# One static order for all engines, and two operands of a two-layer convolution block made by TensorE products instead of a copy through DRAM

## The chip, the core and the metric

The kernel runs on one NeuronCore of a Trainium2 chip. The metric is the device time of one execution in microseconds (us). The core has a matrix engine (TensorE, PE in the profile; its weight loads are listed as PEld), VectorE (DVE), ScalarE (ACT), GpSimd (POOL) and SyncE (SP), which here issues the DMA transfers. [...]

## What is computed

The input x is 32 samples of 96 channels of 56 x 56 values in f32. Two layers follow each other, each with a group normalisation in front (32 groups of 3 channels) and x added at the end.

```python
# layer 0: an inverted bottleneck with 4-bit weights and activations
h = act_q(bn(conv1x1(x, quant_w(w1)) ))          # 96 -> 576 channels
h = act_q(bn(depthwise3x3(h, quant_w(w2))))      # 576
h = bn(conv1x1(h, quant_w(w3)))                  # 576 -> 96
x = x + (gn(x) + h)
# layer 1: three branches of 32 channels, gated by small MLPs of the channels' means
x_0  = group_conv3x3(x_0, conv0_w * Y0)                       # spatial
Mix  = group_conv1x1(frft2d(x_05, alpha), conv05_w * Y)       # fractional Fourier, real and imaginary
x_05 = abs(frft2d(Mix, -alpha)) / (H * W)
x_1  = irfft2(group_conv1x1(rfft2(x_1), conv1_w * Y1))        # Fourier
x = x + conv3x3(concat(x_0, x_05, x_1), conv2_w) + conv2_b    # 96 -> 96
```

## The kernel before

The samples are worked one after the other, with layer 1 of one sample running beside layer 0 of the next. Line numbers are those of the profile.

Layer 0 of a sample. `norm` (L330) takes the channel statistics of x in seven pieces (L333) and `group_stats` (L290) turns them into mean and scale. `split` (L345) writes the normalised x as a high and a low part (`vh`, `vl`). `expand` (L368) makes 128 of the 576 channels at one of four pixel phases: four products on PE (L372), then `quant_act` (L310), in which ScalarE evicts the bank pair to integers (L313) and VectorE clips (L315), then up to four DMAs (L385) that bring the result into the padded buffer `qp`. There are 20 such steps. `depthwise` (L390) is eight fp8 products (L398) for 32 channels with all four phases, and again `quant_act`; 18 such steps. `project` (L407) goes back to 96 channels (L414) and adds to x (L426).

Layer 1 of a sample. `means`, `gates`, `weights` and `angles` (L454 to L605) compute the gates, the sample's own weights `g0`, `g1` and `g2`, and the transform matrices `cs`, a long chain of small steps over PE, VectorE and ScalarE. `mix_t` (L608) and `hilbert` (L624) are the Fourier branch, `spatial` (L722) is the 3 x 3 branch. The fractional branch is the one that the change touches. `mix_f` (L644) multiplies x of that branch by `g1` (`pm`, L653) and gets 128 rows: 64 of them (here called p and q) still have to be transformed, the other 64, called a0 and b0, do not. All 128 go to DRAM (`z`, L658). From there two transfers bring p and q back laid out by image row (`zh`, L663), and eight bring a0 and b0 back laid out by four rows (`az`, L671). `rows_f` (L673) transforms along rows into `Y`, `columns_f` (L694) along columns into the bank `pz` (L702); VectorE adds `az` (L712), ScalarE squares (L713), VectorE adds real and imaginary part into `Z` (L715), and `magnitude` (L717) takes the root into the concatenated image `cat` (L720). `final` (L742) is the last 3 x 3 convolution: for each of seven blocks of eight image rows nine products, called taps, of 96 x 448 from `cat` into one bank (`pc`, L746), then VectorE adds them to x (L754). The profile counts an f32 product as two records.

The order. `interleave` (L87) merges two lists of steps, of layer 0 and of layer 1 of the sample before, by weights written beside each step. The steps are whole functions, so the nine taps of a block stand together. The framework's own scheduler, run with a simulated timeline, may then rearrange instructions. Tiles come from pools with few buffers: two bank pairs for `expand`, `depthwise` and `project`, four single banks for everything else, three buffers for the integers of `quant_act`, three of the clipped `q1s`.

Of the kernel before, what the change touches and what calls it, by code (L numbers as in the profile page):

```python
# [49 lines left out]
NB = 5  # L51
# [12 lines left out]
LEAD = 7  # L64
# [22 lines left out]
def interleave(a, b):  # L87

    ta, tb = sum(c for c, _ in a) or 1, sum(c for c, _ in b) or 1
    i = j = 0  # L90
    ca = cb = 0.0
    while i < len(a) or j < len(b):
        if j >= len(b) or (i < len(a) and ca * tb <= cb * ta):
            ca += a[i][0]
            a[i][1]()
            i += 1
        else:
            cb += b[j][0]
            b[j][1]()
            j += 1  # L100
# [3 lines left out]
def block_kernel(ctx: ExitStack, tc: tile.TileContext, out: bass.AP, a: dict):  # L104
# [5 lines left out]
    xp = ctx.enter_context(tc.tile_pool(name="xp", bufs=3))  # L110
    p1 = ctx.enter_context(tc.tile_pool(name="p1", bufs=1))
    p2 = ctx.enter_context(tc.tile_pool(name="p2", bufs=2))
    p3 = ctx.enter_context(tc.tile_pool(name="p3", bufs=3))
    dp = ctx.enter_context(tc.tile_pool(name="dp", bufs=2, space=bass.MemoryType.DRAM))
    ps0 = ctx.enter_context(tc.tile_pool(name="ps0", bufs=2, space=PSUM))
    ps1 = ctx.enter_context(tc.tile_pool(name="ps1", bufs=4, space=PSUM))

    def bank(pool, name):
        return pool.tile([128, 512], F32, tag="bank", name=name)

    def pair(name):

        return ps0.tile([128, 2, 512], F32, tag="pair", name=name)


    xts = {}

    def load(i):
        xt = xp.tile([C, HW], F32, tag="x", name=f"x{i}")
        nc.sync.dma_start(out=xt, in_=x_in[i].rearrange("c h w -> c (h w)"))  # L130
        xts[i] = xt

    load(0)


# [6 lines left out]
    gmat = const("gmat")  # L142
    def prepare():

        room = p1.tile([128, NG0 * PN // 2], F32, tag="q2", name="prep")
# [107 lines left out]
    for k in range(3):  # L253
        t = cp.tile([128, PH, PW], FP8, tag=f"q1s{k}", name=f"q1s{k}")
        nc.gpsimd.memset(t, 0.0)
        q1s.append(t)
# [17 lines left out]
    bcoef = p1.tile([128, 128], F32, tag="vv", name="bcoef")  # L274
    g1 = cp.tile([128, 128], F32, tag="g1", name="g1")
# [5 lines left out]
    g2 = cp.tile([128, 128], F32, tag="g2", name="g2")  # L281
    nc.vector.memset(g2, 0.0)
    cs = cp.tile([LOW + W, 2 * W], F32, tag="cs", name="cs")
    nc.vector.memset(cs, 0.0)
    zh = cp.tile([LOW + W, G, LOW], F32, tag="zh", name="zh")
    nc.gpsimd.memset(zh, 0.0)
    Y = cp.tile([LOW + W, H, G], F32, tag="Y", name="Y")
    nc.gpsimd.memset(Y, 0.0)

    def group_stats(stats, name):  # L290

        mv = p2.tile([C, 2], F32, tag="mv", name=f"mv{name}")
        nc.vector.bn_aggr(mv, stats)
        pm = bank(ps1, f"pm{name}")
        nc.tensor.matmul(pm[:C, 0:1], gmat, mv[:, 0:1], start=True, stop=True)
        st = p2.tile([C, 4], F32, tag="st", name=f"st{name}")
        mean, rstd, gap, d = (st[:, k : k + 1] for k in range(4))
        nc.vector.tensor_copy(mean, pm[:C, 0:1])
        nc.vector.tensor_tensor(d, mv[:, 0:1], mean, ALU.subtract)
        t = p2.tile([C, 1], F32, tag="gt", name=f"gt{name}")  # L300
        nc.vector.scalar_tensor_tensor(t, d, d, mv[:, 1:2], ALU.mult, ALU.add)
        pv = bank(ps1, f"pv{name}")
        nc.tensor.matmul(pv[:C, 0:1], gmat, t, start=True, stop=True)
        ve = p2.tile([C, 1], F32, tag="ve", name=f"ve{name}")
        nc.vector.tensor_scalar(ve, pv[:C, 0:1], 1e-5, None, ALU.add)
        nc.gpsimd.tensor_tensor(rstd, ve, mhalf, ALU.pow)
        nc.vector.tensor_tensor(gap, d, rstd, ALU.mult)
        return mean, rstd, gap

    def quant_act(ps, scale, offset, dst, name):  # L310

        t = p3.tile([128, PN], I16, tag="qt", name=f"qt{name}")
        nc.scalar.activation(t.rearrange("p (h n) -> p h n", h=2), ps[:, :, :HN], AF.Relu, bias=offset, scale=scale)  # L313
        src = t if len(dst.shape) == 2 else t.rearrange("p (h w) -> p h w", w=PH)
        nc.vector.tensor_scalar(dst, src, 15.0, None, ALU.min, saturate=False if dst.dtype == FP8 else None)  # L315

    stats2 = {}
    turn = {"q1s": 0}


    def phase(xt, k, rows=PH):

        return view(xt, W * (k // 2) + k % 2, [[2 * W, PH], [2, PH]])

    def layer0(i):

        xt = xts[i]
        s = {}

        def norm():  # L330
            stats = p2.tile([C, NCH, 6], F32, tag="bn", name=f"bn{i}")
            for j in range(NCH):
                nc.vector.bn_stats(stats[:, j, :], xt[:, j * CN : (j + 1) * CN])  # L333
            mean, rstd, _ = group_stats(stats.rearrange("p c s -> p (c s)"), f"a{i}")
            s["mean"], s["rstd"] = mean, rstd
            stats2[i] = p2.tile([C, NCH, 6], F32, tag="bn2", name=f"bn2{i}")

            t = p2.tile([C, 3], F32, tag="aff", name=f"aff{i}")
            nmr, s["one"], s["off"] = (t[:, k : k + 1] for k in range(3))
            nc.vector.scalar_tensor_tensor(nmr, mean, -1.0, rstd, ALU.mult, ALU.mult)  # L340
            nc.vector.tensor_scalar(s["one"], rstd, 1.0, None, ALU.add)
            nc.vector.tensor_tensor(s["off"], nmr, B3, ALU.add)
            s["nmr"] = nmr

        def split(k):  # L345
            src = phase(xt, k)
            if k == 0:
                s["vh"] = p1.tile([C, 4, PN], F32R, tag="vh", name=f"vh{i}")
                s["vl"] = p1.tile([C, 4, PN], F32R, tag="vl", name=f"vl{i}")
            for h in range(2):  # L350
                at = slice(HN * h, HN * (h + 1))
                v = p3.tile([C, HN], F32, tag="qt", name=f"v{i}_{k}_{h}")
                nc.vector.tensor_scalar(  # L353
                    v.rearrange("p (h w) -> p h w", w=PH),
                    src[:, PH // 2 * h : PH // 2 * (h + 1), :],
                    s["mean"],
                    s["rstd"],
                    ALU.subtract,
                    ALU.mult,
                )  # L360
                nc.scalar.copy(s["vh"][:, k, at], v)  # L361
                nc.vector.tensor_tensor(s["vl"][:, k, at], v, s["vh"][:, k, at].bitcast(F32), ALU.subtract)

        def base():

            nc.vector.tensor_scalar(xt, xt, s["one"], s["off"], ALU.mult, ALU.add)

        def expand(b, k):  # L368
            ps = pair(f"pe{i}_{b}_{k}")
            for n, v in enumerate((s["vh"], s["vl"])):  # L370
                for h in range(2):
                    nc.tensor.matmul(  # L372
                        ps[:, h, :HN],
                        w1[:, 128 * b : 128 * (b + 1)],
                        v[:, k, HN * h : HN * (h + 1)],
                        start=(n == 0),
                        stop=(n == 1),
                    )
            src = q1s[turn["q1s"] % 3]
            turn["q1s"] += 1  # L380
            quant_act(ps, A1[:, b : b + 1], B1[:, b : b + 1], src[:, :, :PH], f"e{i}_{b}_{k}")

            n, at = blk(b) // G, PW * (k // 2) + k % 2
            for g in range(n):
                nc.sync.dma_start(  # L385
                    out=qps[(NB * i + b) % 3][G * k : G * (k + 1), g, at : at + PH * PW],
                    in_=src[g * G : (g + 1) * G].rearrange("c h w -> c (h w)"),
                )

        def depthwise(b, j):  # L390
            g = 4 * b + j
            if g == 0:
                s["q2"] = p1.tile([128, NG0, PN], BF16, tag="q2", name=f"q2_{i}")
            ps = pair(f"pd{i}_{g}")
            for t in range(4):
                for h in range(2):
# [4 lines left out]
                        view(qps[(NB * i + b) % 3][:, j, :], at, [[PW, PH // 2], [1, PH]]),  # L401
# [3 lines left out]
            quant_act(ps, A2[:, g : g + 1], B2[:, g : g + 1], s["q2"][:, g, :], f"d{i}_{g}")  # L405

        def project(h, lo, hi):  # L407

            if lo == 0:
                s["pp"] = [pair(f"pp{i}_{h}_{u}") for u in range(2)]  # L410
            for g in range(lo, hi):
                for k in range(4):
                    rows = slice(G * k, G * (k + 1))
                    nc.tensor.matmul(  # L414
                        s["pp"][k // 2][:C, k % 2, :HN],
                        w3[rows, g, :],
                        s["q2"][rows, g, HN * h : HN * (h + 1)],
# [3 lines left out]
            if hi < NG0:  # L421
                return
            for k in range(4):
# [4 lines left out]
        def stats():  # L428
            for j in range(NCH):
                nc.vector.bn_stats(stats2[i][:, j, :], xt[:, j * CN : (j + 1) * CN])  # L430
# [542 lines left out]
```

## Time and profile before

| | |
|---|---|
| time, median of 3 runs | 4759.75 us (4745.85 to 4771.58) |
| span of the profiled run | 4750.5 us, mean granted TensorE clock 0.941 |
| final convolution, L746, on PE | 1620.7 us busy, 4032 records |
| depthwise, L398, on PE | 956.8 us busy, 4608 records |
| expand, L372, on PE | 786.4 us busy (434.7 + 351.7), 2560 records |
| evictions of both, L313, on ACT | 1212.3 us busy (635.9 + 576.4) |
| statistics of x, L333, on DVE | 121.1 us busy, 133.6 us idle before them until x had landed |
| DMA | 249.58 MB, 53 GB/s; issues of `qp` 2304, `z` 256, `az` 256, `zh` 64 |

How to read it: "busy" is time in which an engine executes something. A busy PE is not PE at its peak, since the ends of its pipelined products are modelled and since a throttle may grant it half of its clock; the clock row of the page tells. In the list of waits a line names who waited and for whom, then the total in us, the number of times and the longest.

### The profile page before, as it was taken

The numbers are of one execution on the slowest core, as the hardware profiler recorded it, in microseconds if no ns is written. First come the engines' busy times: TensorE is split into PE (matmuls) and PEld (weight loads), VectorE is DVE, ScalarE is ACT, GpSimd is POOL, SyncE is SP. The second block draws the span as 40 slices with busy tenths as digits, with TensorE's granted clock in tenths as the row PEclk, the third lists the DMA queues.
The fourth block names the chain that finished last, engine by engine and source line by source line (L and its number), as shares of the span: only waits on it lengthen the run. The fifth ranks groups of instructions, "written<-read, shape, count | busy, mean of one in ns | idle before, by whom it ended". The sixth has DMA issues, their size and how long they took to land.

```text
span 4750.5 us, 59888 instructions
## 1 busy us (share of the span) xinstructions
PE 4293.0 (90%) x21632; PEld 2471.1 (52%) x21632; DVE 2393.3 (50%) x5385; ACT 2177.6 (46%) x2824; POOL 176.7 (4%) x209
## 2 busy tenths in 40 slices
PE   3799999999998999999999999999999999999987
PEld 2545555545555555555555555455555555555544
DVE  5545545545445455455454455454454554555532
ACT  3534445444455444455444454444454444554431
POOL 1000000000000000000000000000000000000000
PEclk9899999999999999999999999999999999999998
DMA  2212222211223211222211222122222112222112
GB/s 72 44 48 45 42 61 65 64 46 39 48 62 65 62 38 36 59 64 65 58 40 39 58 65 64 43 42 48 62 65 63 35 39 58 65 64 53 33 34 48
DMA packets 397243, 249.58 MB, mean 53 GB/s; under 512 B 283233, under 2 KB 390100, under 8 KB 390804
## 3 DMA queue, kind: packets, MB, share of 16 engines
q1 hardware_dynamic: 394368, 242.76, 23.0%
q8 instruction: 172, 2.82, 0.3%
q10 hardware_dynamic: 2580, 2.99, 0.2%
q14 instruction: 123, 1.01, 0.1%
HBM read 92.90 MB, written 89.92 MB: 38 GB/s over the span
## 4 chain that ended last, share of the span: by engine, by line
PE 63%; DVE 14%; DMA 11%; ACT 6%; issue 4%; SPq 3%; POOL 0%; DVEq 0%; ACTq 0%; POOLq 0%
PE pc L746 31%; PE pd L398 12%; PE pp L414 5%; DMA zh<-z 4%; PE pe L372 4%; PE pm L653 4%; DMA qp<-q1s 3%; PE pi L678 3%; ACT cat L720 2%; SPq L385 2%; DMA z<-zs 2%; DVE bn L333 2%; DVE q1s L315 2%; DVE x L426 2%; DMA x<-in_x_dram 1%
## 5 line engine op out<-in xcount | busy, mean ns | idle before, releaser
L746 PE MATMUL pc<-cat,wc 96*96 96x448 f32 x4032 | 1620.7, 557 | 60.9 <-ACT cat L720 60.9
L746 PEld LDWEIGHTS pc<-cat,wc 96*96 96x96 f32 x4032 | 664.1, 168 | 895.5 <-issue 809.0
L398 PE MATMUL pd<-qp,dw 128*128 128x392 fp8e4 x4608 | 956.8, 353 | 43.0 <-ACT qtd L313 37.9
L313 ACT ACTIVATE qtd<-pd,o,s 128x784 int16<-128x784 f32 x576 | 576.4, 1001 | 908.1 <-PE pd L398 878.2
L313 ACT ACTIVATE qte<-pe,o,s 128x784 int16<-128x784 f32 x640 | 635.9, 998 | 685.3 <-PE pe L372 669.5
L398 PEld LDWEIGHTS <-dw 128*128 128x128 fp8e4 x4608 | 447.4, 102 | 502.2 <-issue 203.9
L372 PE MATMUL pe<-vh,w1r 96*128 96x392 f32 x1280 | 434.7, 422 | 71.1 <-DVE x L426 41.2
L315 DVE TENSOR_SCALAR q1s<-qte 128x784 fp8e4<-128x784 int16 x640 | 358.8, 562 | 240.4 <-ACT qte L313 144.3
L315 DVE TENSOR_SCALAR q<-qtd 128x784 bf16<-128x784 int16 x576 | 207.0, 359 | 499.1 <-ACT qtd L313 496.4
L754 DVE SCALAR_TENSOR_TENSOR x<-pc,bc,x 96x448 f32<-96x448 f32 x224 | 152.0, 679 | 582.7 <-PE pc L746 581.2
L372 PE MATMUL pe<-vl,w1r 96*128 96x392 f32 x1280 | 351.7, 357 | 0.0
L372 PEld LDWEIGHTS pe<-vh,w1r 96*128 96x128 f32 x1280 | 221.8, 198 | 222.2 <-issue 94.9
L653 PE MATMUL pm<-xf,g 34*128 34x392 f32 x512 | 202.7, 768 | 107.5 <-DVE bn L333 105.0
L414 PE MATMUL pp<-q,w3q 32*96 32x392 bf16 x4608 | 255.8, 327 | 2.2 <-DVE x L426 2.2
L372 PEld LDWEIGHTS pe<-vl,w1r 96*128 96x128 f32 x1280 | 246.1, 198 | 0.5
L426 DVE SCALAR_TENSOR_TENSOR x<-pp,s,x 96x392 f32<-96x392 f32 x256 | 142.2, 616 | 175.8 <-PE pp L414 175.8
L414 PEld LDWEIGHTS <-w3q 32*96 32x96 bf16 x4608 | 182.0, 118 | 84.6 <-issue 31.5
L726 PE MATMUL ps<-xq,g 128*128 128x392 f32 x512 | 201.1, 536 | 0.0
L678 PE MATMUL pi<-cs,zh 120*120 120x112 f32 x1024 | 136.9, 295 | 63.8 <-DMA zh<-z 57.9
L333 DVE BATCH_NORM_STATS2 bn<-x 96x6 f32<-96x448 f32 x224 | 121.1, 608 | 133.6 <-DMA x<-in_x_dram 133.6
L361 ACT CAST vh<-v 96x392 fp32r<-96x392 f32 x256 | 126.2, 516 | 128.7 <-DVE v L353 127.9
L678 PEld LDWEIGHTS pi<-cs,zh 120*120 120x120 f32 x1024 | 131.6, 209 | 75.6 <-DVE cat L640 24.1
(149 smaller groups left out, 3881.5 us busy)
## 6 DMA issues: line engine op xcount, KB each, us to landing
qp<-q1s SPq DMA_DIRECT2D x2304, 26.2 KB
z<-zs SPq DMA_DIRECT2D x256, 196.0 KB
x<-in_x_dram SPq DMA_DIRECT2D x32, 1176.0 KB
out_dram<-x SPq DMA_DIRECT2D x32, 1176.0 KB
zh<-z SPq DMA_DIRECT2D x64, 392.0 KB
az<-z SPq DMA_DIRECT2D x256, 98.0 KB
xf<-vv SPq DMA_DIRECT2D x128, 6.1 KB
prep<-in_w_dram ACTq DMA_DIRECT2D x1, 864.0 KB
```

Of the source, the lines that this page charges most:

```text
L313: nc.scalar.activation(t.rearrange("p (h n) -> p h n", h=2), ps[:, :, :HN], AF.Relu, bias=offset, scale=scale)
L315: nc.vector.tensor_scalar(dst, src, 15.0, None, ALU.min, saturate=False if dst.dtype == FP8 else None)
L333: nc.vector.bn_stats(stats[:, j, :], xt[:, j * CN : (j + 1) * CN])
L372: nc.tensor.matmul(ps[:, h, :HN], w1[:, 128 * b : 128 * (b + 1)], v[:, k, HN * h : HN * (h + 1)], start=(n == 0), stop=(n == 1),)
L398: nc.tensor.matmul(ps[:, h, :HN], dw[:, g, t, :], view(qps[(NB * i + b) % 3][:, j, :], at, [[PW, PH // 2], [1, PH]]), start=(t == 0), stop ...
L414: nc.tensor.matmul(s["pp"][k // 2][:C, k % 2, :HN], w3[rows, g, :], s["q2"][rows, g, HN * h : HN * (h + 1)], start=(g == 0), stop=(g == NG ...
L426: nc.vector.scalar_tensor_tensor(part, src, A3, part, ALU.mult, ALU.add)
L653: nc.tensor.matmul(ps[:, :HN], g1[rows], s["xf"][rows, at], start=True, stop=True)
L678: nc.tensor.matmul(ps[: LOW + W, 2 * W * k : 2 * W * (k + 1)], zh[:, c : c + 2, :].rearrange("p c w -> p (c w)")[:, : LOW + W], cs, start= ...
L726: nc.tensor.matmul(ps[:, :HN], s["g0"][:, 128 * k : 128 * (k + 1)], view(xq, PH // 2 * h * (W + 2) + k, [[W + 2, PH // 2], [2, PH]]), star ...
L746: nc.tensor.matmul(ps[:C, :CN], wc[:, C * t : C * (t + 1)], cat[:, CR * j + dy : CR * j + dy + CR, dx : dx + W], start=(t == 0), stop=(t = ...
L754: nc.vector.scalar_tensor_tensor(part, ps[:C, :CN], bc, part, ALU.add, ALU.add)
```

## The change

It has two parts. The first is the order. Every step of the kernel (in places single instructions, such as one tap) is no longer carried out when it is met, but handed to a `Plan`: with its engine, an estimated cost, what it reads and writes, and which bank or buffer it takes or gives back. `Plan.run` is a list scheduler: it computes for each step the longest remaining path within its sample, gives earlier samples a bonus, simulates all five queues and the pools, and at each point lets the engine that can start earliest take the ready step of highest rank. Steps are then issued in that order, and the framework is told to keep it. All tiles are allocated once, as fixed buffers; `q1s` has five instead of three, the integers of `quant_act` four instead of three. The taps of several row blocks may be under way in several banks at once.

The second part is the fractional branch. `mix_f` now makes only p and q (64 rows). For a0 and b0, x of that branch is also laid out by four rows (`x4`, four copies with normalisation), their weights are put into a block-diagonal matrix `g4`, and two products per bank in `columns_f` write a0 and b0 into the very bank in which the column transform then accumulates. The copy `az` and the addition on VectorE go, and ScalarE squares straight from the bank. The transfers `zh` become four of half the size, two as soon as each half of `z` is written, and `magnitude` works in two halves.

The core of the diff:

```diff
-def interleave(a, b):
...
+class Plan:
+    LAT = {"PE": 0.5, "ACT": 0.3, "DVE": 0.3, "POOL": 0.4, "SP": 1.9}
+    KEEP = 1.0
...
+        for p in reversed(self.steps):
+            p["rank"] = p["cost"] + max([gap(p, q) + q["rank"] for q in p["succ"] if q["sample"] == p["sample"]], default=0.0)
+        for p in self.steps:
+            p["key"] = (-(p["rank"] + (samples - p["sample"]) * PERIOD), p["n"])
...
+                    start = max(e["t"], self.steps[n]["at"])
+                    for slot in self.steps[n]["take"] or ():
...
+                        start = max(start, ends[want - 1][0] if want <= len(ends) else math.inf)
+                    if start < math.inf and (best is None or (start, key) < best[:2]):
+                        best = (start, key, n, e)
...
+        order.sort(key=lambda p: (p["start"], p["n"]))
...
+        for p in order:
+            p["f"]()
...
+        plan.add(i, "PE", 0.95, product, reads=parts, writes=[key, ("q1s", e % NQ)], take=[tok])
...
+            plan.add(
+                i, "SP", 0.6, lambda g=g: move(g), reads=[("q1s", e % NQ)], writes=[("qp", (NB * i + b) % 3, g, k)], lat=1.8
+            )
...
-                ps = bank(ps1, f"pm{i}_{j}_{h}")
-                nc.tensor.matmul(ps[:, :HN], g1[rows], s["xf"][rows, at], start=True, stop=True)
...
-            for r in range(4):
-                for t in range(2):
-                    src = z[2 * G + G * t : 3 * G + G * t].rearrange("o (q r w) -> r o q w", r=4, w=W)
-                    nc.sync.dma_start(out=az[G * r : G * (r + 1), :, t, :], in_=src[r])
...
+                nc.tensor.matmul(banks[tok["k"]][:64, :HN], g1[rows], xf[rows, HN * k : HN * (k + 1)], start=True, stop=True)
...
+                    add("SP", 0.6, get, reads=[("z", i % 2, 4 * h + q) for q in range(4)], writes=[("zh", h, r)], lat=4.0)
...
+            nc.vector.tensor_reduce(
+                g4[at, :, at], view(tmpf[at], 256, [[128, 2], [4, 32], [1, 4]]), AX.X, ALU.add
+            )
...
             def columns_f(g=g, m=m, tok=tok):
+                ps = banks[tok["k"]]
+                for t in range(2):
+                    nc.tensor.matmul(
+                        view(ps, W * t, [[2 * W, m], [1, W]]),
+                        g4[:, t, :],
+                        x4[:, 4 * W * g : 4 * W * g + W * m],
+                        start=(t == 0),
+                        stop=False,
+                    )
...
-            add = s["az"][:, 4 * g : 4 * g + n].rearrange("p q t w -> p (q t w)")
-            nc.vector.tensor_tensor(sq[:, :m], ps[:, :m], add, ALU.add)
-            nc.scalar.activation(sq[:, :m], sq[:, :m], AF.Square)
+                nc.scalar.activation(sq[t["k"]][:, : 2 * W * m], banks[tok["k"]][:, : 2 * W * m], AF.Square)
...
+            for t in range(9):
+                add("PE", 0.755, lambda t=t, f=tap: f(t), reads=deps, writes=[("pc", i, j)], take=[tok] if t == 0 else None)
...
-        interleave(conv, one[:-4])
-        interleave(now["last"], one[-4:-2])
...
+    with tc.manual_schedule(engines={engines.PE, engines.Activation, engines.DVE, engines.Pool, engines.SP}):
+        plan.run(B)
...
-    with tile.TileContext(nc, schedule_with_timeline_sim=True) as tc:
+    with tile.TileContext(nc) as tc:
```

## The prediction

> **What bounds the kernel now.** I read, in this order: the page's busy shares and clock row, the busy time by stretch, TensorE's waits, and the time around its longest repeated wait. First the page:
>
> ```profile
> PE 4293.0 (90%) x21632; PEld 2471.1 (52%) x21632; DVE 2393.3 (50%) x5385; ACT 2177.6 (46%) x2824; POOL 176.7 (4%) x209
> PEclk9899999999999999999999999999999999999998
> DMA  2212222211223211222211222122222112222112
> ```
>
> TensorE (PE) is the only engine near its span; VectorE and ScalarE are half idle and DMA is at a fifth. The clock row shows a second loss: it is 9, not 10. The view of cores gives a mean clock of 0.941, so 0.059 x 4750.5 = 280 us of full speed were not granted. Busy time by stretch (start, the long middle, the end; columns: stretch, us, then busy us and instructions of PE, PEld, DVE, ACT, POOL, then clock, DMA share, GB/s):
>
> ```profile
> 0.00:110.00 110.00, 40.87 (x173) 27.78 (x174) 61.17 (x157) 37.46 (x45) 22.91 (x19) 1.00 0.30 76
> 110.00:345.00 235.00, 200.01 (x1061) 119.17 (x1058) 123.11 (x277) 112.42 (x142) 10.06 (x11) 0.88 0.18 43
> 345.00:4595.00 4250.00, 3931.41 (x19918) 2258.31 (x19916) 2163.11 (x4854) 1999.39 (x2595) 139.48 (x174) 0.95 0.24 53
> 4595.00:4692.40 97.40, 70.05 (x359) 44.35 (x358) 39.93 (x89) 27.14 (x42) 4.26 (x5) 0.75 0.22 46
> 4692.40:4750.50 58.10, 50.64 (x126) 21.45 (x126) 6.00 (x9) 1.21 (x2) 0.00 (x0) 0.91 0.07 21
> ```
>
> PE is idle 104 us in the first 345, 319 in the middle (29.5 samples of 144 us, so 10.8 a sample), 35 at the end. Who ended those idle times:
>
> ```profile
> PE pm L653 <- DVE bn L333: 105.0, 29, 4.3
> PE pc L746 <- ACT cat L720: 60.9, 32, 6.7
> PE pi L678 <- DMA zh<-z: 57.9, 27, 5.0
> PE pe L372 <- DVE x L426: 41.2, 31, 1.3
> PE pd L398 <- ACT qtd L313: 37.9, 77, 4.9
> PE pmb L295 <- DVE mvb L293: 31.8, 31, 4.8
> ```
>
> About one wait of each kind per sample: a repeated bubble, not a slow engine. The largest, once a sample, looked at closely (same columns):
>
> ```profile
> 2100.00:2199.90 99.90, 94.50 (x482) 51.15 (x480) 50.77 (x110) 45.95 (x55) 4.26 (x5) 1.00 0.14 36
> 2199.90:2203.30 3.40, 0.07 (x2) 0.07 (x1) 3.40 (x8) 1.25 (x2) 0.00 (x0) 1.00 0.03 6
> 2203.30:2217.00 13.70, 13.70 (x36) 5.50 (x36) 4.80 (x12) 4.45 (x6) 0.00 (x0) 0.50 0.33 110
> 2217.00:2244.00 27.00, 25.66 (x167) 19.73 (x165) 16.20 (x42) 17.59 (x30) 0.55 (x1) 1.00 0.59 95
> ```
>
> PE stood still for 3.4 us and then worked 13.7 us at half speed: the gap costs 3.4 + 13.7/2 = 10.2 us. The timeline shows what happened beside it:
>
> ```profile
> 2199.41 3.78 DVE L333 BATCH_NORM_STATS2 bn<-x 96x6 f32<-96x448 f32 x7 [3.94 <-DMA x<-in_x_dram]
> 2199.45 3.26 SPq L603 DMA_DIRECT2D xf<-vv  x4
> 2203.26 1.50 PE L653 MATMUL pm<-xf,g 34*128 34x392 f32 x2 [3.33 <-DVE bn L333]
> ```
>
> VectorE, after waiting for the next sample's x, took seven statistics in a row, and the first `pm` is put down to them; but in the same 3.8 us the rows `xf<-vv`, which `pm` also needs, were issued and landed, so both may have held it. What matters: PE's next instruction in order was `pm`, and no independent work stood ahead of it. So the bound is PE's work plus bubbles plus the clock that the bubbles cost.
>
> [...] every half-speed piece that I looked at follows a window with PE clearly underused, as above. [...]
>
> **The change part by part.**
> 1. *PE's work at full speed.* Busy 4293.0. Of the 280 us of lost clock some fell on idle time (13.70 of 13.70 us were busy in the stretch above, less at the end); I take 263. Work: 4293 - 263 = 4030 us, 126 a sample. It stays.
> 2. *Added: a0 and b0 by products.* For each group of 4 row quads two products of 224 columns, for the last group two of 112: 3 x 448 + 224 = 1568 columns a sample. Price from the chain: 18 `pc` records of 448 columns take 6.77 us, 0.376 each, and an f32 product is two records, so 448 columns cost 0.752. That is 3 x 0.752 + 0.376 = 2.63 us a sample, 84 in all. If none of their 16 weight loads (209 ns, row L678 PEld) hid, 16 x 0.209 = 3.34 a sample, 107 in all. I take 87, as loads hide behind the taps today. All on PE, so all on the path. Work after: 4117.
> 3. *Removed: the copy.* 8 `az` issues of 98 KB a sample and half of the 196 KB of each `z` write. No PE wait in the list names `az`, and DMA is at 0.24: worth nothing directly. Indirectly the 7.3 us in which SyncE issued `az` right behind `zh` go, and `zh` no longer shares the engines with it (57.9 us of waits). SyncE falls from 96 to 90 issues a sample, at about 0.6 us some 54 of 130 us: not a bound.
> 4. *VectorE and ScalarE.* Gone: the add L712, 72.2. The two reductions for g1 halve, from 42.9 to about 26 (410 ns each, the row L542). Added: 128 reductions for g4 at 0.41 = 52, 64 copies of x4 on VectorE at half of L490's 1.086 = 35. Sum near 0. ScalarE: 64 x4 copies at 0.87 = 55 and roots in eight pieces instead of four, about 30; 2178 becomes 2263. Both stay near 53% of the shorter span. The square now reads the bank directly, one hop less.
> 5. *The order.* The old order mixes two lists by weights in lumps (a final convolution row block is 18 records, 6.8 us), then lets a scheduler rearrange. The new one places single taps (0.75 us). In the changed program's PE order of a middle sample one tap stands after every two depthwise products, single taps stand between expands, and about 45 taps run through the stretch of means and gates, with the small products strung between them. So each wait of the list above has independent PE work beside it; the rows `xf<-vv` get their own priced step (0.6 + 2.0 us), and x's statistics are placed when x has landed. Its estimates err to the safe side: it allows 0.3 us from ScalarE to VectorE, where the timeline has an eviction ending at 2131.56 and the clip starting at 2131.59; it prices a tap at 0.755 (measured 0.752). What it may misjudge is DMA: `zh` first issued at 2222.36, its consumer starting at 2230.44, is 8.1 us for two full transfers with `az` beside; it allows 0.6 + 4.0 for a half. Bound: 0 to 3.5 us of PE a sample. New waits are all on slots of the same kind; behind a PE instruction that waits stand all its taps, which is why a misjudged place would cost a gap.
>  Of the 10.8 us idle a sample I keep a quarter, 2.7, 80 us over the middle. With gaps that short the half speed all but goes: of some 210 us lost in the middle (0.05 x 4250) I keep 20.
> 6. *Start and end.* Weight preparation, its DMA and the first sample's convolution without a partner stay: 104 idle becomes 90. At the end the previous sample's taps now fill the last sample's chain: 35 becomes 15. Half speed there: 15.
>
> Sum: 4117 + 80 + 20 + 90 + 15 + 15 = 4337; I say 4335.
>
> **The rivals.** *Half the bubbles come back elsewhere* (a bank, a slot, `zh`): 4117 + 160 + 130 clock + 120 start and end = 4527. For it: four banks must hold taps, spatial and spectral results at once, and taps of three or four row blocks keep banks for long. Against: VectorE and ScalarE, which free them, are half idle. *Everything fits*: 4117 + 105 + 15 = 4237, and less by up to 45 if the modelled ends of products before gaps (a `pd` record shows 0.353 us where records follow each other every 0.17; some 270 waits are listed) were never work; against it, no fixed order meets real DMA times exactly. *Slower*: the fixed order blocks as often as before (458 us idle, clock 0.94) and the products come on top: 4750 + 87 = 4837, more if blocking is worse. For it: [...] `pm` in the timeline shows what one bad place costs. Against: the estimates lie close to the measured rows.
>
> **How the numbers follow.** First case (4260 to 4450) 0.68; half back (4450 to 4700) 0.19; everything fits (under 4260) 0.08; slower 0.05. Predicted is the first, 4335. The range 4210 to 4530 leaves out half of the second, the far end of the third and the last. Faster by over 0.5% 0.93, within 0.5% 0.02, slower 0.05.
>
> **What would show it.** PE busy near 4150 with a clock of 0.98 or more (steps 1, 2, 5); the products' new row near 85 us; the wait of `pm` for statistics gone and no wait of PE over about 40 us in sum outside the start (step 5); idle in the first 345 us still near 90 (step 6). Wrong: a clock still at 0.95, or a new repeated PE wait on a slot or on `zh` of over 3 us a sample.

## The result and the profile after

The kernel after takes 4590.76 us (median; 4569.37 to 4594.77) against 4758.95 before (four runs; the three above gave 4759.75): a ratio of 0.9642, with a 95% interval of 0.9606 to 0.9677. It is faster, by 168 us, but that is 40% of the gain that I forecast (4335), and the time lies outside the range.

The page of the kernel after, its busy shares and clock row:

```profile
PE 4357.0 (95%) x22144; PEld 2484.4 (54%) x22144; DVE 2434.4 (53%) x5450; ACT 2278.1 (50%) x3012; POOL 194.6 (4%) x211
PEclk9998899999999999999999999999999999999999
```

PE's share rose from 90 to 95%, and the clock is still a 9 (its mean went from 0.941 to 0.955). The stretches of the kernel after (columns as before: stretch, us, busy us and instructions of PE, PEld, DVE, ACT, POOL, clock, DMA share, GB/s):

```profile
0.00:110.00 110.00, 36.27 (x145) 25.34 (x145) 72.24 (x170) 35.20 (x45) 40.59 (x22) 1.00 0.30 74
110.00:345.00 235.00, 219.52 (x1331) 129.52 (x1332) 133.69 (x302) 136.57 (x166) 10.54 (x11) 0.94 0.12 27
345.00:4450.00 4105.00, 3992.54 (x20306) 2275.83 (x20305) 2204.94 (x4931) 2088.39 (x2765) 143.47 (x178) 0.96 0.19 44
4450.00:4567.60 117.60, 108.69 (x366) 53.66 (x364) 23.52 (x49) 17.90 (x37) 0.00 (x0) 0.92 0.14 35
```

Idle time of PE is 89 us in the first 345, 112 in the middle, 9 at the end: 210.6 instead of 457.5. Its longest waits now:

```profile
PE bank L416 <- DVE mva L413: 46.1, 5, 38.6
PE pair L519 <- ACT vh L485: 29.4, 3, 25.0
PE bank L811 <- DMA xf<-vv: 28.9, 8, 4.8
```

The first two are mostly the start (their longest alone is 38.6 and 25.0); the next ones are under 20. The once-a-sample wait for statistics is gone. So the gaps closed much as forecast, and yet the clock came back only in small part. Where it was lost is seen in a stretch without any gap:

```profile
540.90:547.80 6.90, 6.90 (x23) 2.54 (x21) 5.22 (x16) 2.53 (x6) 0.55 (x1) 1.00 0.08 17
547.80:568.30 20.50, 20.50 (x44) 11.82 (x43) 11.23 (x22) 9.68 (x14) 0.00 (x0) 0.50 0.14 36
```

PE was busy for all of 6.90 us and was then given half speed for 20.5 us. The timeline of PE in the last part of that stretch (start, us, engine, line, operation, records):

```profile
544.24 1.53 PE L811 MATMUL bank<-xf,g 34*64 34x392 f32 x4
545.70 0.99 PE L1010 MATMUL bank<-cat,wc 96*96 96x448 f32 x2
546.62 1.74 PE L811 MATMUL bank<-xf,g 34*64 34x392 f32 x4
```

and the same products (`mix_f`) in the kernel before:

```profile
1925.18 0.93 PE L653 MATMUL pm<-xf,g 34*128 34x392 f32 x4
```

Four records are two products. Before, the two were the two halves of the image, on partitions 0 to 33 and 64 to 97 of their tiles: their records start 6 ns apart, they ran at once, and the pair took 0.93 us. After, the steps of `mix_f` are ordered by half (four of the first, then four of the second), two products next to each other lie on the same partitions, their records start some 330 ns apart, and they take 1.53 us one after the other (the second four records take 1.74, as the last of them runs into the half speed). In these traces the two on different partitions overlapped, and those on the same ones did not.

The accounts of all kernels below are worked out from the records in one way: *work* is PE's busy time with the part at half speed counted half, *loss* is that other half, *idle* the rest. All three are of the one profiled run, the time is the median of four.

| kernel | median us | ratio, interval | span | work | idle | loss |
|---|---|---|---|---|---|---|
| before | 4758.95 | 1 | 4750.5 | 4030 | 458 | 263 |
| forecast | | | 4337 | 4117 | 185 | 35 |
| after | 4590.76 | 0.9642 (0.9606 to 0.9677) | 4567.6 | 4165 | 211 | 192 |
| pairs | 4487.73 | 0.9438 (0.9415 to 0.9461) | 4485.5 | 4080 | 240 | 165 |
| wide2 | 4608.54 | 0.9690 (0.9662 to 0.9717) | 4601.0 | 4175 | 206 | 220 |
| rows98 | 4582.23 | 0.9633 (0.9602 to 0.9663) | 4584.3 | 4180 | 239 | 166 |
| rows64 | 4585.61 | 0.9642 (0.9622 to 0.9662) | 4579.2 | 4172 | 253 | 155 |
| products_only | 4866.74 | 1.0235 (1.0212 to 1.0258) | 4867.5 | 4104 | 391 | 372 |
| order_only | 4599.02 | 0.9672 (0.9652 to 0.9692) | 4597.9 | 4059 | 263 | 276 |
| order_pairs | 4579.63 | 0.9609 (0.9567 to 0.9651) | 4581.7 | 4014 | 311 | 257 |
| pairs_small | 4659.43 | 0.9802 (0.9778 to 0.9826) | 4656.5 | 4103 | 304 | 249 |
| block | 4373.87 | 0.9197 (0.9163 to 0.9232) | 4365.4 | 4055 | 217 | 93 |
| block_rows | 4349.58 | 0.9142 (0.9113 to 0.9171) | 4350.8 | 4052 | 220 | 79 |
| pad | 4332.24 | 0.9102 (0.9087 to 0.9117) | 4333.1 | 4049 | 226 | 59 |
| pad_lat | 4403.53 | 0.9241 (0.9208 to 0.9275) | 4400.7 | 4047 | 270 | 83 |

### The profile page after: what moved, and what is told of

It reads as the page before. It is cut to its first block, busy times and chain, and to the rows that moved or that the text cites. A ratio compares the mean times of both kernels' runs of the same rounds, so it can differ in the third digit from the quotient of the medians.

```text
span 4567.6 us, 60927 instructions
## 1 busy us (share of the span) xinstructions
PE 4357.0 (95%) x22144; PEld 2484.4 (54%) x22144; DVE 2434.4 (53%) x5450; ACT 2278.1 (50%) x3012; POOL 194.6 (4%) x211
## 4 chain that ended last, share of the span: by engine, by line
PE 83%; DVE 5%; ACT 4%; SPq 3%; DMA 3%; issue 2%; ACTq 0%; DVEq 0%; POOL 0%; POOLq 0%
PE bank L1010 34%; PE pair L558 16%; PE pair L519 9%; PE pair L586 5%; PE bank L811 5%; PE bank L873 4%; SPq L530 3%; PE bank L934 2%; PE bank L789 2%; PE bank L962 2%; PE bank L971 2%; ACT qt L502 1%; PE bank L907 1%; PE bank L910 1%; DMA zh<-z 1%
## 5 line engine op out<-in xcount | busy, mean ns | idle before, releaser
L1010 PE MATMUL bank<-cat,wc 96*96 96x448 f32 x4032 | 1772.6, 563 | 32.1 <-ACT cat L998 19.6
L502 ACT ACTIVATE qt<-pair,o,s 128x784 int16<-128x784 f32 x1216 | 1209.3, 1004 | 739.4 <-PE pair L558 373.3
L1010 PEld LDWEIGHTS bank<-cat,wc 96*96 96x96 f32 x4032 | 638.5, 168 | 627.9 <-issue 558.8
L558 PE MATMUL pair<-qp,dw 128*128 128x392 fp8e4 x4608 | 881.7, 342 | 5.3 <-ACT qt L502 3.2
L507 DVE TENSOR_SCALAR q1s<-qt 128x784 fp8e4<-128x784 int16 x640 | 362.3, 569 | 516.8 <-ACT qt L502 306.5
L519 PE MATMUL pair<-vh,w1r 96*128 96x392 f32 x1280 | 509.1, 480 | 50.6 <-ACT vh L485 29.4
L519 PEld LDWEIGHTS pair<-vh,w1r 96*128 96x128 f32 x1280 | 241.9, 200 | 264.4 <-issue 153.3
L519 PE MATMUL pair<-vl,w1r 96*128 96x392 f32 x1280 | 352.7, 358 | 0.2
L586 PE MATMUL pair<-q,w3q 32*96 32x392 bf16 x4608 | 269.1, 338 | 1.5 <-ACT qt L502 1.4
L519 PEld LDWEIGHTS pair<-vl,w1r 96*128 96x128 f32 x1280 | 250.6, 200 | 2.7 <-DVE vl L488 2.5
```

What stands on the lines that cost most here:

```text
L519: nc.tensor.matmul(ps[:, h, :HN], w1[:, 128 * b : 128 * (b + 1)], v[:, k, HN * h : HN * (h + 1)], start=(n == 0), stop=(n == 1),)
L558: nc.tensor.matmul(ps[:, h, :HN], dw[:, g, t, :], view(qp[:, j, :], at, [[PW, PH // 2], [1, PH]]), start=(t == 0), stop=(t == 3),)
L586: nc.tensor.matmul(pairs[toks[k // 2]["k"]][:C, k % 2, :HN], w3[rows, g, :], q2[rows, g, HN * h : HN * (h + 1)], start=(g == 0), stop=(g = ...
L1010: nc.tensor.matmul(banks[tok["k"]][:C, :CN], wc[:, C * t : C * (t + 1)], cat[:, CR * j + dy : CR * j + dy + CR, dx : dx + W], start=(t == ...
```

## The experiments

My theory after the result (A): the order took `mix_f` apart, which costs work, and products that sum over few rows bring the half speed even with PE busy. Rivals: it is the number of columns; it is only gaps; it is the new products.

Two terms. A half-speed *piece* is a stretch in which half of the clock was granted. It stands *behind a busy window* where PE was busy for at least three quarters of the 3.41 us before it, otherwise *behind a gap*. In the kernel before all 72 pieces (564 us) stand behind gaps. In after 20 (195 us) stand behind busy windows and 29 (214 us) behind gaps, so each sort makes up about half of the loss of 192. The diffs below are shortened.

**Pairs: undo the split of `mix_f`.**

```diff
-for j in range(8): h, k = divmod(j, 4)   # one step per half and block
-    add("PE", 0.68, mix_f, ..., take=[tok])
+for k in range(4):                       # one step makes both halves, two banks
+    add("PE", 0.86, mix_f, ..., take=toks)
```

> The kernel after, with one edit: the two halves of mix_f (rows 0 to 33 and rows 64 to 97 of the array) are one step of the scheduler again, their products next to each other as in the kernel before; nothing is left out. Theory A (the order put the halves one after the other[...]: that costs some 64 us of work and is what the half-speed stretches follow that come after fully busy windows): a pair of products takes about 0.86 us instead of 1.3, mix_f's work falls from 190 to about 130 us at full speed, the half-speed pieces behind busy windows go (some 50 to 100 us), clock 0.975 or more, time 4430 to 4490. Theory B (the half speed comes of something else: the columns in use, or gaps): the work falls by 60 or less but the clock stays near 0.955, time 4530 to 4560.

Measured 4487.73, 103 us less than after and within the range; work fell by 84 us, `mix_f` from 190 to 113 us at full speed. That part of A is shown. The clock of 0.975 is not: the pieces behind busy windows fell from 195 to 75 us, but those behind gaps rose from 214 to 303, so it reached 0.958 only. (The waits for `zh` rose from 3.5 to 34.5 us. I read it so that the first half of `z` is now complete hardly before the second; that wasn't tried.) The row of `mix_f` among the groups of pairs:

```profile
L811 PE MATMUL bank<-xf,g 34*64 34x392 f32 x512 | 138.5, 566 | 8.9 <-DVE cs L686 4.2 <-DVE zs L819 1.4 <-ACT cat L891 1.1
```

and that of after (the first number behind the bar is busy us, then mean ns of a record, then idle time before it and who ended it):

```profile
L811 PE MATMUL bank<-xf,g 34*64 34x392 f32 x512 | 241.0, 591 | 31.1 <-DMA xf<-vv 28.9 <-ACT zs L814 1.6 <-DVE zs L814 0.5
```

**Wide2: twice the columns (and two small copies a sample on VectorE, which make them).**

```diff
-matmul(bank[:64, :HN], g1[rows, 64 columns], xf[rows, ...])
+matmul(bank[:, :HN], g1[rows, 128 columns], xf[rows, ...])
```

> The kernel after, with one edit: mix_f's weights have 128 columns again (its 64 columns twice, by a small copy on DVE per half; the upper 64 output rows go unused), its eight products still one after the other. Nothing of the output is left out. If the half speed behind busy windows follows the number of columns in use (34 x 64 against 34 x 128), it goes: clock 0.975 or more, 4490 to 4530. If it follows the rows in use, or that products stand alone (theory A), nothing changes: clock near 0.955, the time within 20 us of the kernel after's (about 4591).

4608.54, 18 us above after and within the 20 expected, with a loss of 220 against 192: no better. PE's instructions come in the same order as in after. So the 64 columns were not what brought the half speed.

**The parts alone.**

```diff
 # order_only: after, with a0 and b0 from mix_f by copies
+for r in range(4): for t in range(2): add("SP", 0.6, get_az, ...)
-NQ = 5; zs x 4; products into the columns' bank
+NQ = 4; zs x 3; add az on DVE
 # products_only: before, with x4, g4 and the products; no az
```

> Part 1 of the change alone: the list scheduler, with a0 and b0 made by mix_f (128 columns) and copied by eight DMAs as before, added on DVE; two pools of buffers one smaller to make room. mix_f's products one after the other, as the scheduler puts them. Nothing is left out. Theory A (the order brings the serial mix_f): the 99 us of the products leave, PE work about 4070, the half-speed pieces behind busy windows stay, clock 0.955 to 0.965, time about 4480 to 4520. If the products of part 2 cause the half speed, the clock rises to 0.98 and the time is about 4380. If the copy of a0 and b0 makes the path wait again, the PE idle returns to over 300 us and the time is 4580 or more.

> Part 2 of the change alone: the order of the kernel before (mix_f in pairs), but a0 and b0 made by the products in the columns' bank from x laid out by 4 rows, and no copy of them. Nothing is left out. My working: the products add 87 to 110 us of PE work and the copy was not on the path, so 4840 to 4870 if the gaps stay as they are. If the shorter SP queue and the missing wait on the copies close some gaps, 4780 to 4830. If it is under 4750, the copy did bound the kernel before and step 3 of the prediction is wrong. With mix_f in pairs, theory A expects no half speed behind fully busy windows here.

Products alone cost 114 us in the old order (4866.74). That is in the expected range, but by luck: work rose by 74 us only, idle time fell by 66 and the loss rose by 109, and I have not followed that up. Two of its 71 half-speed pieces (17 us) stand behind busy windows, so the new products by themselves don't bring that sort. The order alone gives 4599.02, about the same as both parts together, though it has 106 us less work: its idle time and loss are 136 us higher. It has 21 pieces (171 us) behind busy windows, without any of the new products. None of its three cases fits as a whole: the time is that of the third, but idle time (263) stays under 300. Its pools are smaller than those of after, and the runs of the buffers below show what that can cost.

**Kinds: what the clock follows.** A measuring kernel, run once; the computation is left out, and single kinds of products run in stages, each behind taps. K is the number of rows that a product sums over, which is the number of rows of its weights.

> A measuring kernel, not a version of this one: all of the computation is left out (it sends x to the output) and TensorE runs stages of some 40 us of one kind of product each, from the kernel's own shapes, each stage behind 31 us of the taps' products: first 13 kinds back to back with the taps, then the same 13 kinds behind a wait of some 5 us, then taps alone behind waits of eight lengths; all twice. It tells what the granted clock follows. Theory A (the clock follows how much of the array is in use per window of about 3.4 us): with no wait at all, the stages of mix_f in single products (34 x 64) and of the K = 1 products fall to half speed and stay there; taps, depthwise and spatial stages do not; behind a wait, the taps are back at full speed after one or two windows (3 to 7 us) while the stages of low use stay at half speed to their end. Theory B (only idle time of TensorE counts): no stage without a wait falls to half speed, and behind a wait all kinds come back after the same time. The 34 x 128 stages tell whether columns count; the stages in pairs whether two row groups count together.

Stages of 34 x 64 products with no wait ahead, K = 1 products with no wait, then behind a wait of 4.4 us: taps, 34 x 64 in the same order, 34 x 64 in pairs, and row transforms of 120 rows:

```profile
159.30:180.00 20.70, 20.70 (x114) 10.15 (x113) 0.00 (x0) 0.00 (x0) 0.00 (x0) 1.00 0.94 275
385.90:447.20 61.30, 61.30 (x302) 61.18 (x301) 0.00 (x0) 0.00 (x0) 0.00 (x0) 0.53 0.00 1
943.80:974.00 30.20, 30.20 (x75) 12.95 (x76) 0.00 (x0) 0.00 (x0) 0.00 (x0) 0.92 0.00 0
1020.40:1060.50 40.10, 40.10 (x114) 15.71 (x113) 0.00 (x0) 0.00 (x0) 0.00 (x0) 0.50 0.00 0
1097.80:1160.70 62.90, 62.90 (x193) 22.26 (x193) 0.00 (x0) 0.00 (x0) 0.00 (x0) 0.50 0.00 0
1693.90:1734.50 40.60, 40.60 (x361) 40.60 (x362) 0.00 (x0) 0.00 (x0) 0.00 (x0) 0.93 0.01 1
```

In this run K = 1 products fell to half speed without any gap (0.53 over 61.3 us). The 34-row products didn't (1.00 over 20.7 us; here my stage missed its aim: with four of one half, then four of the other and nothing between, they overlapped, 0.37 us each), but once a wait had brought half speed they didn't leave it before the stage ended (0.50 for 40 and 63 us), while taps and 120-row products were back after 5 to 6 us (0.92 and 0.93 over their stretches). "Only idle time counts" is out.

What this is a picture of can be counted. All half-speed pieces lie on a fixed grid of 3.41 us (the 72 of before and the 49 of after start whole multiples of 3.413 us apart). For each window of that grid I took as use the sum of (rows of weights / 128) x (the product's time at full speed), over 3.41 us (128 is the most rows that a product of these kernels has), for kinds, before, after, pairs and products_only together, without each kernel's start:

```
use of the window    next window at half speed
under 0.35               761 of  761
0.35 to 0.38              65 of  199
0.38 to 0.40               5 of   51
0.40 to 0.45               7 of  209
0.45 and more              0 of 5292
```

Counted a second way, with each record priced by its columns, the step lies some 0.02 higher, and 2 of 5371 windows from 0.45 on are followed by half speed. By that count half speed followed 10 of 10 full-speed windows in which PE was busy for 95% or more and use was under 0.35, and none of 4783 such windows with a use of 0.45 or more. So in these kernels the clock followed the rows in use and not whether PE was busy. By the same count taps (96 rows) have 0.75 at full speed and 0.375 at half, just enough to leave it, as they did after 5 us; a pair of `mix_f` has 0.53 and 0.27, and did not leave it in 63 us; a stream of single ones has 0.27 at full speed. The window 544.4 to 547.8 above has 3.5 single products and one tap: (3.5 x 0.65 x 34/128 + 0.75 x 96/128)/3.41 = 0.34.

**Rows98 and rows64: the same products over more rows, the added ones zero.**

```diff
-matmul(..., g1[34 rows], xf[34 rows])
+matmul(..., g1h[98 rows, other half zero], xf[98 rows])    # rows98
+matmul(..., g1[64 rows, 30 zero], xf[64 rows])             # rows64
```

> The kernel after, in the same order and with mix_f's eight products still one after the other, but each contracts over 98 rows instead of 34: the weights of the other half's rows (and of the 30 rows between) are zero, so the values are the same. Nothing is left out. Theory A, sharpened by the measuring kernel: windows of 3.41 us in which (rows of weights x columns streamed) is under some 0.36 of 128 rows at full speed are followed by half speed. Then the work stays (mix_f about 190 us at full speed, 4165 in all) and only the clock gets better: most of the 195 us of half-speed pieces behind busy windows goes, and pieces behind gaps get shorter; half-speed loss 192 to about 110 to 130, time 4510 to 4545. If rows of zeros don't count, or if it is the order of the products and not their rows, the time is within 20 us of 4591.

> The kernel after with its order untouched instruction for instruction: each product of mix_f only contracts over 64 rows instead of 34, the 30 more of them zero, so no wait, no dependency and no value changes (rows98 had changed what mix_f waits for, and with it the order and the gaps). Nothing is left out. Theory A (rows of weights x columns streamed under some 0.36 of the array per window brings the half speed): a single mix_f product now uses 0.5 of the rows; work stays at 4165 and gaps at 210, the half-speed pieces behind busy windows fall from 20 (195 us) to those behind the K = 1 products (about 7, 35 us), and some pieces behind gaps get shorter; half-speed loss 192 to 90 to 120, time 4490 to 4525. If rows of zeros don't count, or the half speed was a matter of the order alone: within 15 us of 4591.

The clock did as the count says: behind busy windows 20 pieces (195 us) became 7 (34 us) and 8 (38 us), so rows of zeros counted. But the time did not move (4582.23, 4585.61): both miss the time that A gave, and by the time alone the rival had it. It is the pieces, in rows64 with the order unchanged, that decide between the two. Why was no time gained? rows98 had changed what waits for what, and so the order; rows64 has the order of after, so it can be compared stretch by stretch. For one sample, the section from the first `mix_f` to its last, and from there to the first row transform, in the stretches of after:

```profile
544.20:562.80 18.60, 18.60 (x43) 9.85 (x42) 14.43 (x31) 11.38 (x18) 0.17 (x1) 0.60 0.13 32
562.80:613.20 50.40, 49.79 (x227) 30.93 (x226) 15.85 (x34) 28.38 (x30) 0.00 (x0) 0.95 0.31 60
```

The same section of rows64:

```profile
541.30:553.60 12.30, 12.02 (x43) 5.98 (x42) 12.21 (x28) 10.56 (x18) 0.10 (x1) 1.00 0.14 32
553.60:607.30 53.70, 47.27 (x227) 29.57 (x226) 17.39 (x37) 29.10 (x31) 0.00 (x0) 0.99 0.30 60
```

`mix_f` is done 6.3 us sooner, and 3.3 us of that are lost again before the row transform, in a wait for `zh` of 5.6 us; behind it the clock is 0.77 for the next 11.7 us. SyncE's queue in rows64 (start, us, issues), and below it that of after:

```profile
552.80 37.31 SPq L532 DMA_DIRECT2D qp<-q1s  x57
590.16 2.51 SPq L819 DMA_DIRECT2D z<-zs  x4
598.19 1.18 SPq L819 DMA_DIRECT2D z<-zs  x2
599.42 2.95 SPq L830 DMA_DIRECT2D zh<-z  x4
```

```profile
595.35 2.72 SPq L817 DMA_DIRECT2D z<-zs  x4
605.03 3.12 SPq L828 DMA_DIRECT2D zh<-z  x4
```

The four stores of `z` at 590.16, whose data lay ready from 554, stand in the fixed order behind at least 57 issues of `qp` (37.31 us), and the last two results wait for the buffers that they free (their copies start at 592.4 and 593.1). In after the same stores went out at 595.35, long after `mix_f` had ended there, too. I read it so that in this section SyncE's queue sets the pace and PE's half speed had been filling a wait; with a shorter queue it wasn't tried. Over the kernel idle time rose by 42 us and the loss behind gaps by 43; together they ate the 78 gained. Of the 42, waits for `zh` (3.5 to 18.2 us) and for `zs` (14.9 to 27.8) make up 28; the rest isn't traced.

**Block: both halves of `mix_f` in one product.**

```diff
-2 products of 34 rows x 64 columns, 2 banks, 2 copies
+1 product of 98 rows x 128 columns (block diagonal), 1 bank, 1 copy
```

> The kernel after, but mix_f makes both halves in one product: weights of 98 rows x 128 columns with the two halves' 34 x 64 on the diagonal and zeros elsewhere (four products a sample instead of eight, one bank and one copy of 128 partitions instead of two of 64). Nothing is left out. Theory A: mix_f's work 4 x 32 x 0.65 = 84 us instead of 190 (pairs: 113), so 4165 - 106 = 4060 of work, and no low-use windows of mix_f: half-speed loss 120 to 150, gaps 210 to 240: time 4400 to 4450. If single products with 98 rows still bring the half speed, the loss stays near 190 and the time is about 4480.

4373.87, under the expected range: work is 4055 as expected, the loss 93 and not 120 to 150. `mix_f` is four products of 98 rows a sample instead of eight, with half the copies, 93 us at full speed. Its row (256 records instead of 512):

```profile
L812 PE MATMUL bank<-xf,g 98*128 98x392 f32 x256 | 123.0, 582 | 62.7 <-DMA xf<-vv 61.1 <-ACT zs L815 1.1 <-ACT xq L863 0.3
```

Pieces behind busy windows are 10 (38 us), about as many as in rows64, and those behind gaps fell to 174 us. The order is another one than that of after.

**Block_rows and pad: more rows of zeros in the K = 1 products, then in taps and expansion.** PE's order is the same in block, block_rows and pad.

```diff
-row = sb([1, ...])                        +row = sb([128, ...]), zeroed          # block_rows
-cat, wc, vh, vl, w1: 96 partitions        +128 partitions, 32 of them zero       # pad
```

> The kernel block, with the K = 1 outer products of the gates made over 128 rows, 127 of them zero (the row tile gets 128 partitions, zeroed once). Nothing is left out. In the kernel pairs 16 half-speed pieces (75 us, so 37 lost) stood behind windows with twelve of these products. Theory A: those pieces go, 15 to 37 us faster than block. If it is the rows with values that count, or the number of small products, the same time as block within 10 us.

> The kernel block_rows with the two longest low-row products filled up to 128 rows by rows of zeros: the taps (96 rows) and the expansion (96 rows). Nothing is left out. Half-speed loss in block_rows is 79 us, all of it behind windows with gaps. Theory A: with full rows at full speed a window bears a longer gap before it falls under 0.36 (2.2 us of 3.4 instead of 1.8), and at half speed a full window counts 0.5 instead of 0.375, so the stretches end sooner: loss 79 to 45 to 60, time 4315 to 4340. If only idle time counts, the same time as block_rows (4350) within 10 us.

4349.58 and 4332.24: 24 and 17 us less, within both expectations, with no value and no place in PE's order changed. All 10 pieces behind busy windows went with the first. The intervals of block_rows and pad just touch, but the loss in the records fell with each step (93, 79, 59) while work and idle time stayed within 9 us. The mean clock of pad is 0.983. Pad is faster than before and after: 0.9102 (0.9087 to 0.9117).

**Order_pairs and pairs_small: what part 2 is worth.**

```diff
 # order_pairs: order_only with mix_f in pairs
 # pairs_small: pairs, with order_only's pools
-NQ = 5; zs x 4
+NQ = 4; zs x 3
```

> Part 1 alone (the kernel order_only: list scheduler, a0 and b0 by mix_f and by copies), with mix_f's two halves as one step in pairs, as in the kernel pairs; nothing is left out. Beside pairs it tells what part 2 is worth once mix_f is in pairs. From the products alone (94 to 99 us of PE work that leave) it would be 4488 - 95 = 4393; if the copies and DVE's additions bring back as much in gaps and half speed as in order_only against after (gaps +52, half-speed loss +84), it is 4480 to 4540, and part 2 pays for itself under the list scheduler only.

> The kernel pairs (part 2's products, mix_f in pairs) with the two pools of buffers as small as order_pairs has them: four buffers of the quantised expansion instead of five, three of mix_f's results instead of four. Nothing is left out. order_pairs, without part 2, took 92 us more than pairs though it has about 66 us less PE work. If the smaller pools did that, this kernel loses most of it: 4560 to 4660, with waits at mix_f for zs and at the depthwise products for qt as in order_pairs. If the copies of a0 and b0 and the additions on DVE did it, this kernel stays within 25 us of pairs (4488).

Order_pairs (4579.63) lies above all that I had allowed, pairs_small (4659.43) at the upper edge of its first case. With equal small pools the kernel with the products takes 80 us more than the one with the copies. Its work is 89 us more, its idle time and loss together 13 less: about the products' price, and the copies cost next to nothing against it, as far as two kernels with different orders can show. With the larger pools it takes 172 less (4487.73). So under the list scheduler part 2 pays, as I read it, by the room that it leaves for one buffer more in each of two pools: `az` held 6.3 KB a partition, and `x4` and `g4` take 4.2 of them. The waits of pairs_small that pairs does not have at this size:

```profile
PE pair L558 <- ACT qt L502: 43.7, 47, 3.1
PE bank L811 <- ACT zs L819: 29.0, 15, 5.2
PE bank L811 <- DVE zs L819: 22.4, 12, 4.6
```

In pairs they are 7.3, 0.7 and 1.4. Smaller pools also change the order as a whole, and the 172 us are not divided further.

**Pad_lat: one planned latency.**

```diff
-add("SP", 0.6, place_v, ..., lat=2.0)
+add("SP", 0.6, place_v, ..., lat=6.0)
```

> The kernel pad with one number changed: the scheduler is told that the four small copies of v into xf land 6.0 us after their issue instead of 2.0. Nothing is left out. In pad TensorE waits 59 us at mix_f for these copies, in 16 waits of 3.7 us, the largest of its waits behind the start, and each is as long as a window of the clock. If the gaps that are left come of the planned latencies (theory A's account of the rest), that wait falls under 15 us, the half-speed loss from 59 to 35 to 45, and the time to 4255 to 4295. If the order finds other gaps instead, 4320 to 4345.

4403.53: slower, which neither case had. The wait that it aimed at went from 59.3 to 4.3 us, but the one for `zh`, 5.8 us in pad, took its place:

```profile
PE bank L945 <- DMA zh<-z: 47.1, 8, 10.6
PE bank L819 <- DMA xf<-vv: 4.3, 3, 2.1
```

One number moves the whole order, here by 71 us. So tens of us between kernels with different orders are not by themselves evidence; the comparisons in one order (rows64 and wide2 with after, block_rows and pad with block) are the clean ones.

## Why the prediction was wrong

The profiled kernel after is 231 us over my sum of 4337: work +48, idle +26, loss +157. The step that failed most is the last sentence of step 5, on the half speed; step 1 failed as well.

*Step 1, the work stays (4030):* failed by `mix_f`, which went from 125 to 190 us at full speed. I carried its cost over without asking what had stood beside it. The other kinds together became 28 us less (among them taps +31, expansion -31, depthwise -12, spatial +14), which I had not foreseen either. Pairs brought `mix_f` down to 113, and the time down by 103.

*Step 2, the products (87, between 84 and 107):* right. 99 us in the records; 89 of work and 80 of time between the two kernels with equal pools.

*Step 3, the copy worth nothing:* right for the copy itself as far as the kernels with equal pools show, but I overlooked what its room is worth: the list scheduler lives on buffers, and two fewer cost 172 us in pairs.

*Step 4, VectorE near 0, ScalarE +85:* DVE rose by 41 us, ACT by 100; neither sets the end.

*Step 5, the order:* its first half held (112 us idle in the middle, against 80; no repeated wait over 40 us but those of the start). What failed is the sentence "with gaps that short the half speed all but goes". I had 35 us of loss, the profile has 192, and a clock still at 0.95, which the prediction named as a sign of being wrong, is about what came (0.955). Two things were wrong in it, and each makes up about half of the loss. I took the half speed to follow idle time alone, as all 72 pieces of before stand behind gaps; that short gaps would bring next to none was my estimate, and no run had shown it. What counted in the measurements was rows in use, and the new order, which strings low-row products together, makes such windows with PE busy (20 pieces, 195 us). And by the count of windows above I estimate that a gap of some 1.8 us is long enough when the rest of the window is taps: 0.75 x (3.41 - 1.8)/3.41 = 0.35. In the measuring kernel a wait of 0.80 us among taps cost no half speed (1.00 over the next 30 us), one of 1.62 us was followed by 3.4 us of it (0.94). There are fewer pieces behind gaps than before, 29 instead of 72, but each lasts about as long (7.4 us, before 7.8).

The loss was not to be had back as time by the clock alone: rows64 gave full speed back behind the busy windows and got no time; that SyncE's fixed queue held these sections is read from one of them, not tried. With fewer and fuller products the time came (block, 217 us less than after: work 110, loss 99 less), though in another order.

*Step 6, start and end:* 89 us idle in the first 345 (90 forecast), 9 at the end (15).

Of the rivals, "half the bubbles come back" had 4527 and named banks and `zh`; its time is nearer, its reason is not what happened. What is left of idle time in pad (226) I can only describe: about 70 of it is the start, 59 are waits at `mix_f` for `xf<-vv`, the rest is spread over small waits. Waits for transfers whose place in the fixed order doesn't fit are still there, and pad_lat did not mend them.

## What to carry to other kernels

Before a reordering is priced by its gaps, look at which products now stand next to each other: the products of `mix_f` on different partitions took 113 us as neighbours (pairs) and 190 us apart (after). Count rows in use, not busy time, when half speed is at stake: a product over few rows can be filled up with rows of zeros (24 us less in block_rows, a further 17 in pad), or two can share one block-diagonal product (93 us instead of 190 for `mix_f` in block), without a change of value. And under a static order compare only kernels whose order is the same, or allow some 70 us of 4330 for the shuffle alone (one case, pad_lat).

## What the runs showed of the hardware that I had not expected

- By the first count half speed followed each of 761 windows of 3.41 us in which rows in use x time, as a share of 128 rows, was under 0.35, 65 of 199 from 0.35 to 0.38, and none of 5292 from 0.45 on. With 128 columns instead of 64 the loss was no smaller (wide2, 220 us against 192), and rows of zeros counted like others (rows64: 20 pieces behind busy windows became 8, in the same order).
- It held itself: eight `pd` records took 2.79 us at half speed and 1.55 at full (before), so the same products count about half. Pairs of 34-row products stayed at half speed (0.50) for 63 us to the end of their stage, and in a stage without a wait they ran 32 us at full speed (1.00) without falling (kinds).
- Filling rows with zeros cost no time on PE here: the outer products took 46.7 us busy with 1 row (block) and 44.8 with 128 (block_rows), the taps stayed at 1562 us at full speed from 96 to 128 rows (block_rows, pad).
